# Graph network of four layers on one core: layer 0 with its sums two blocks ahead of its lists, and gathers that wait for the fourth gather ahead

## The chip, the cores and the metric

The kernel runs on one core of a Trainium2 chip. The metric is the device time of one launch in microseconds; lower is better. A core has five instruction streams that run beside each other and meet through semaphores: PE (matrix products), DVE (VectorE), ACT (ScalarE), POOL (GpSimd, which here issues the gathers) and SP (which issues plain loads). Each stream is in program order.

## What is computed

There are 3327 nodes with 256 features and an adjacency matrix of 3327 x 3327 integers, about 16 ones in a row. Layer 0 is an attention whose score depends on the row alone, so that its softmax has only two weights in a row, one for neighbours and one for the others:

```python
h = x @ Wt.T + bt
s = leaky_relu(h @ Wa.T + ba, 0.2)
w = softmax(where(adj > 0, s, NEG), axis=1)
y = x + (w @ h) @ Wp.T + bp
x = gamma * (y - mean(y)) * rsqrt(var(y) + EPS) + beta
```

Layers 1 to 3 are transformer layers over the neighbours of each node, with eight heads:

```python
q, k, v = layer_norm(x) @ w_qkv
x = x + softmax(where(adj != 0, q @ k.T * SCALE, -inf)) @ v @ w_proj + b_proj
x = x + gelu(layer_norm(x) @ w1 + b1) @ w2 + b2
```

## The kernel before

The nodes are 26 blocks of 128 rows (the last has 127). Four consecutive blocks are a group; the seventh group has two. All engines' orders are written out by hand: what the Python code calls first comes first in each engine's stream.

**Layer 0** reads the adjacency matrix once and does two things with it. The first is the *lists*: of each row the numbers of its neighbours, at most 40. VectorE multiplies a block's row of zeros and ones with column numbers (`candidates`, one product and 16 searches for the eight largest of a segment), and then takes the largest of these (`list`, five searches and four replacements). The second is the *sums*: the sum of h over a row's neighbours, and their number. For it PE turns the block (`turn`: 26 transposes, which ScalarE copies back from PSUM in four pieces to `s_aT`), and two turned blocks at a time are multiplied with h, split into three bf16 parts (`Group.sums`, L843 and L845).

When a group's sums are complete, twelve steps follow: `copy` and `back` bring the sums back to rows (`s_acc`), `soft` takes the number of neighbours (`deg`, L882) and each node's place in an ordering by this number (`places`, `rank`) and the two softmax weights, `mix` and `project` give the update, `add` and `norm` the normalized row, `norm1`, `turn1`, `qkv` the first transformer layer's queries, keys and values, and `store` writes them. Keys and values go to `kv1`, in the order of the nodes, everything else to `t1`.

The order: block 0 is loaded and turned, then `setup` computes h of all nodes (`x_turn`, `h_of`), with VectorE and ScalarE sharing the copies. Then block i+1 is loaded and block i turned; after two blocks their sums are made; and the steps of a finished group wait in a list `late`, from which `some` takes one before `candidates`, one before `list` and one after it. A load's tail columns are cleared on GpSimd (L702), which at the start has 26 gathers of x in its stream. After the last block, the permutation `perm` that sorts the nodes by their number of neighbours is worked out from the ranks, in between the last group's steps.

**Layers 1 to 3** go through the blocks in the sorted order, so that a block's rows have about equally many neighbours. `gather_rows` (L1186) fetches a block's row of `t1`; `issue` (L1226) fetches keys and values of one neighbour of each of the 128 rows: one gather on GpSimd, 270 KB in layer 1 and 262 KB after it, up to four for one buffer, of which there are ten. A gather waits for its buffer, and for the completion of the eighth indirect transfer ahead of it, whose semaphore it uses again. VectorE makes scores from the keys (L1248, L1249) and weighs the values (L1289), PE adds these up (L1294) and does the dense part.

Of the kernel before, what the change touches and what calls it, by code (L numbers as in the profile page):

```python
# [17 lines left out]
P = 128  # L18
N = 3327
# [43 lines left out]
FAR = 2.0 ** 100  # L63

# [459 lines left out]
def sparse_path(ctx, tc, ins, out, dram, flag):  # L524
# [98 lines left out]
    with tc.tile_pool(name="a", bufs=1) as a, tc.tile_pool(name="aw", bufs=2) as aw, \  # L623
# [42 lines left out]
        nrow = 3 * D + 2 * H0 + 1  # L666
        row = a.tile([1, nrow], FP, name="s_row")
        o = 0
        for name, n in (("gamma", D), ("beta", D), ("bp", D), ("bt", H0), ("Wa", H0), ("ba", 1)):
            src = ins[f"L0_gnn_{name}"]  # L670
            nc.sync.dma_start(row[:, o:o + n], src if len(src.shape) == 2 else src[None, :])
            o += n
# [15 lines left out]
        places = a_acc.tile([P, 512], FP, tag="places", name="places")  # L688

        class Block:  # L690
# [5 lines left out]
            def load(self):  # L696
                i, r = self.i, self.r
                a32 = aw.tile([P, N], I32, tag="a32", bufs=3, name=f"s_a32_{i}")
                for p0, p1 in (((0, P),) if r == P else ((0, r // 16 * 16), (r // 16 * 16, r))):
                    nc.sync.dma_start(a32[p0:p1], ins["adj"][i * P + p0:i * P + p1, :])  # L700
                self.abf = aw.tile([P, PADDED], BF, tag="abf", bufs=3, name=f"s_abf_{i}")
                nc.gpsimd.memset(self.abf[:, N:], 0.0)  # L702
                if r < P:
                    nc.gpsimd.memset(self.abf[96:P, :], 0.0)
                nc.scalar.sign(self.abf[:r, :N], a32[:r])
# [11 lines left out]
            def candidates(self):  # L717
                i = self.i
                v = aw.tile([P, NSEG, SEG], BF, tag="v", name=f"s_v_{i}")
                nc.vector.tensor_mul(v, self.abf.rearrange("p (s c) -> p s c", c=SEG),  # L720
                                     seg1[:, None, :].to_broadcast([P, NSEG, SEG]))
                self.cand = aw.tile([P, NSEG, 8], FP, tag="cand", name=f"cand_{i}")
                for s in range(NSEG):
                    nc.vector.max(out=self.cand[:, s, :], in_=v[:, s, :])  # L724
# [15 lines left out]
        def setup():  # L740

            wtT = a.tile([P, 2, H0], FP, name="s_wtT")
            S.wpT = a.tile([H0, D], FP, name="s_wpT")
# [5 lines left out]
            nc.vector.tensor_copy(wtT, pt[:, :2 * H0].rearrange("p (c h) -> p c h", c=2))  # L749
            nc.vector.tensor_copy(S.wpT, pt2[:H0, :D])  # L750
# [7 lines left out]
            S.gam_b, S.bet_b, S.bp_b = (brow[:, k * D:(k + 1) * D] for k in range(3))  # L758
            bt_b = brow[:, 3 * D:3 * D + H0]
            wa_b = brow[:, 3 * D + H0:3 * D + 2 * H0]  # L760
            ba_b = brow[:, nrow - 1:nrow]

            h_sb = aw.tile([P, NB, H0], FP, tag="abf", bufs=3, name="s_h")
            nc.vector.memset(h_sb[96:P, NB - 1, :], 0.0)
            turned = {}

            def x_turn(g):
                blocks = GROUPS[g]
                xT = aw.tile([P, 2, 512], FP, tag="hT", name=f"s_xT_{g}")
                for c in range(2):  # L770
                    pb = bank(f"s_px_{g}_{c}")
                    for j, i in enumerate(blocks):
                        nc.tensor.transpose(pb[:, j * P:(j + 1) * P],
                                            x_sb[:, i, c * P:(c + 1) * P], ident)
                    (nc.vector.tensor_copy if c else nc.scalar.copy)(
                        xT[:, c, :len(blocks) * P], pb[:, :len(blocks) * P])
                turned[g] = xT

            def h_of(g):
                blocks, xT = GROUPS[g], turned.pop(g)  # L780
                ph = bank(f"s_ph_{g}").rearrange("p (b h) -> p b h", h=H0)
                for j, i in enumerate(blocks):
                    for c in range(2):
                        nc.tensor.matmul(ph[:, j, :], xT[:, c, j * P:(j + 1) * P],
                                         wtT[:, c, :], start=(c == 0), stop=(c == 1))
                full = [j for j, i in enumerate(blocks) if ROWS[i] == P]
                for j0, j1, r in ((0, len(full), P), (len(full), len(blocks), ROWS[-1])):
                    if j1 > j0:
                        i0 = blocks[j0]
                        nc.vector.tensor_add(  # L790
                            h_sb[:r, i0:i0 + j1 - j0, :], ph[:r, j0:j1, :],
                            bt_b[:r, None, :].to_broadcast([r, j1 - j0, H0]))

            for g in range(len(GROUPS)):
                x_turn(g)
                if g:
                    h_of(g - 1)
            h_of(len(GROUPS) - 1)

# [3 lines left out]
            nc.vector.tensor_copy(hs[:, :, :H0], h_sb)  # L805
            nc.vector.tensor_sub(rest, h_sb, hs[:, :, :H0])
            nc.vector.tensor_copy(hs[:, :, H0:2 * H0], rest)
            nc.vector.tensor_sub(rest, rest, hs[:, :, H0:2 * H0])
            nc.vector.tensor_copy(hs[:, :, 2 * H0:3 * H0], rest)
            S.fold = a.tile([P, H0], FP, name="s_fold")  # L810
            nc.vector.tensor_copy(S.fold, ident[:, :H0])
            nc.vector.tensor_add(S.fold, S.fold, ident[:, H0:])

            ph = bank("s_phsum")
            for i in range(NB):
                r = ROWS[i]
                nc.tensor.matmul(ph[:, :H0], ones[:r, :], h_sb[:r, i, :],
# [4 lines left out]

            nc.vector.tensor_mul(rest, h_sb, wa_b[:, None, :].to_broadcast([P, NB, H0]))
            s = S.s = a.tile([P, NB], FP, name="s_s")
            nc.vector.tensor_reduce(s, rest, AX.X, ALU.add)
            nc.vector.tensor_scalar(s, s, ba_b, None, ALU.add)
            nc.vector.scalar_tensor_tensor(s, s, 0.2, s, ALU.mult, ALU.max)

        class Group:
# [17 lines left out]

            def steps(self):
                return [self.copy, self.back, self.soft, self.mix, self.project, self.add,
                        self.norm, self.norm1, self.turn1, lambda: self.qkv(0),  # L850
                        lambda: self.qkv(2), self.store]
# [19 lines left out]
            def soft(self):  # L871
# [4 lines left out]
                def sv(name):  # L876
# [10 lines left out]
                                        top[:, :, None].to_broadcast([P, n, nd]), ALU.is_equal)  # L887
                for j in range(n):
                    i = b0 + j
                    nc.tensor.matmul(places[:, :nd], tri, OH[:, i, :], start=(i == 0), stop=True,  # L890
                                     skip_group_check=True)
                    t = aw.tile([P, nd], FP, tag="place", name=f"place_{i}")
                    nc.vector.tensor_mul(t, places[:, :nd], OH[:, i, :])
                    nc.vector.tensor_reduce(rank[:, i:i + 1], t, AX.X, ALU.add)
                    nc.tensor.matmul(places[:, :nd], rest_tri, OH[:, i, :], start=False, stop=True,
                                     skip_group_check=True)
# [36 lines left out]
            def project(self):  # L933
# [4 lines left out]
                nT = aw.tile([H0, 512], FP, tag="nT", bufs=1, name=f"s_nT_{g}")  # L938
                nc.scalar.copy(nT[:, :n * P], pt[:H0, :n * P])
                self.ps = []  # L940
                for j0 in range(0, n, 2):
                    ps = bank(f"s_pp_{g}_{j0}").rearrange("p (b d) -> p b d", d=D)
                    for j in range(2):
                        nc.tensor.matmul(ps[:, j, :], ones[0:1, :], row[:, 2 * D:3 * D],
# [623 lines left out]
```

## Time and profile before

| | us |
|---|---|
| time, median of three runs | 2890.99 (2877.77 to 2891.98) |
| span of the profiled run | 2886.5 |
| first row gather of layer 1 (L1186) starts | 630.1 |
| last gather of layer 3 starts | 2789.1 |
| VectorE busy in the whole span | 1981.0 |
| PE busy in the whole span | 2003.6 |
| GpSimd: 1344 gathers of keys and values, one of them | 1273.2, 0.947 |
| VectorE: 416 searches of `candidates`, one of them (L724) | 117.5, 0.360 |
| ScalarE: 104 copies of turned pieces, one of them (L715) | 83.3, 0.853 |

How to read it: the page gives each engine's busy time and, in 40 slices of 72 us, its busy share in tenths. A busy share tells little alone: an engine with 70% can be the bound of a stage if its work is in a chain with that of others. So the idle time matters, and what ended it: a row such as "DVE deg L882 <- ACT s_acc L869: 92.8, 6, 19.1" says that VectorE's instruction of line 882 was waited for in all 92.8 us, six times, 19.1 at most, until ScalarE's instruction of line 869 was done. In a timeline each row has its start, its duration, engine, line, operation, output and inputs, and in brackets the idle time before it and what ended it.

### The profile page before, as it was taken

The page shows a single profiled execution, that of the slowest core. Times are in us where ns is not written, and L with a number is a line of the kernel's source. Part 1 is how long each engine was busy: PE and PEld are TensorE (multiplying, and loading weights), DVE is VectorE, ACT ScalarE, POOL GpSimd, SP SyncE. Part 2 cuts the span into 40 slices and gives each one's busy share as a digit, 9 for nine tenths or more (in the row PEclk, how much of TensorE's full clock was granted, in tenths as well). Part 3 has the DMA queues.
Part 4 walks back from the last instruction along what each step waited for, and adds up shares of the span by engine and source line. Part 5 has one row for each costly group of instructions (what it writes and reads, how often), then busy time and mean ns, then how long its engine had stood idle before and what let it go on. Part 6 is the DMA issues. An engine that isn't in the chain of part 4 may idle for free. (4 is left out here: it accounts for less than half of the span.)

```text
span 2886.5 us, 21905 instructions
## 1 busy us (share of the span) xinstructions
PE 2003.6 (69%) x6391; PEld 1062.0 (37%) x6391; DVE 1981.0 (69%) x4141; ACT 791.8 (27%) x1363; POOL 1359.1 (47%) x1461
## 2 busy tenths in 40 slices
PE   4566666623678887897347878878782678777866
PEld 4344444411334333344213434333350233333334
DVE  2977787447787777773378877777714886778852
ACT  2443443200233332332102323332230023222221
POOL 3000000017776766650377655665405777777740
PEclk9677666756889989898678989988995798888988
DMA  4323331137776766670477656665506776666650
GB/s 179 128 98 119 125 104 52 52 112 217 217 220 197 210 197 188 181 180 16 144 210 210 194 174 178 190 181 155 120 27 189 210 202 194 190 190 188 200 135 15
DMA packets 144480, 453.67 MB, mean 157 GB/s; under 512 B 29522, under 2 KB 40157, under 8 KB 141022
## 3 DMA queue, kind: packets, MB, share of 16 engines
q0 software_dynamic: 113056, 370.26, 45.7%
q1 hardware_dynamic: 9834, 53.90, 5.3%
q10 hardware_dynamic: 21458, 28.02, 2.7%
q8 instruction: 52, 0.85, 0.1%
q14 instruction: 80, 0.65, 0.1%
HBM read 420.64 MB, written 31.42 MB: 157 GB/s over the span
## 5 line engine op out<-in xcount | busy, mean ns | idle before, releaser
L1226 POOL DMA_INDIRECT kv<-kv,t x1344 | 1273.2, 947 | 806.0 <-issue 370.0
L1294 PE MATMUL po<-vw,s_ident 128*128 128x512 f32 (+1 forms) x1380 | 778.2, 700 | 493.5 <-DVE vw L1289 443.6
L1248 DVE TENSOR_TENSOR kv<-kv,q 128x1024 f32<-128x1024 f32 (+3 forms) x363 | 413.4, 1139 | 309.7 <-DMA kv<-kv,t 152.9
L1294 PEld LDWEIGHTS po<-vw,s_ident 128*128 128x128 f32 x1380 | 286.3, 221 | 845.3 <-issue 476.5
L1249 DVE TENSOR_REDUCE sc<-kv 128x32 f32<-128x1024 f32 (+3 forms) x363 | 414.1, 1141 | 12.4
L1289 DVE TENSOR_TENSOR vw<-kv,w 128x1024 f32<-128x1024 f32 x333 | 371.2, 1127 | 0.2
L1373 PE MATMUL pu<-fT,s_w 128*128 128x512 f32 (+3 forms) x768 | 302.4, 527 | 1.0 <-ACT fT L596 1.0
L1396 PE MATMUL py<-gT,s_w 128*128 128x512 f32 (+2 forms) x672 | 283.8, 549 | 0.0
L1379 ACT ACTIVATE gT<-pu,pvb 128x512 f32<-128x512 f32 (+3 forms) x192 | 116.6, 608 | 350.7 <-PE pu L1373 350.2
L702 POOL MEMSET s_abf<- 128x1 bf16 x26 | 2.6, 104 | 435.2 <-PE s_ptb L714 251.6
L1373 PEld LDWEIGHTS pu<-fT,s_w 128*128 128x128 f32 x768 | 147.4, 201 | 136.2 <-issue 111.6
L1396 PEld LDWEIGHTS py<-gT,s_w 128*128 128x128 f32 x672 | 127.8, 192 | 123.1 <-issue 105.4
L714 PE MATMUL s_ptb<-s_ident_bf,s_abf 128*128 128x128 bf16 x676 | 76.5, 291 | 115.7 <-ACT s_aT L715 84.4
L724 DVE MAX8 cand<-s_v 128x8 f32<-128x208 bf16 x416 | 117.5, 360 | 0.9
L714 PEld LDWEIGHTS <-s_abf 128*128 128x128 bf16 x676 | 65.4, 135 | 128.9 <-issue 94.7
L1426 PE MATMUL pk<-s_w_qkv,nT 128*128 128x512 f32 x208 | 106.4, 636 | 8.8 <-ACT nT L596 8.8
L588 ACT ACTIVATE xn_f<-t,nm_f,rqy_f 128x256 f32<-128x256 f32 x78 | 42.9, 593 | 247.6 <-DVE nm_f L582 238.3
L1263 ACT ACTIVATE sc<-sc,mx 128x120 f32<-128x120 f32 (+6 forms) x78 | 31.9, 410 | 260.9 <-DVE mx L1260 257.1
L1334 DVE TENSOR_TENSOR t<-t,po 128x256 f32<-128x256 f32 x78 | 32.5, 417 | 99.7 <-PE po L1330 95.2
L715 ACT COPY s_aT<-s_ptb 128x896 bf16<-128x896 bf16 x104 | 83.3, 853 | 64.6 <-PE s_ptb L714 64.6
L1186 POOL DMA_INDIRECT t<-t,perm x26 | 24.6, 946 | 158.6 <-DMA colsb<-in_L_gnn_be_dram 151.0
L1414 DVE TENSOR_TENSOR t<-t,pd 128x256 f32<-128x256 f32 x75 | 29.5, 408 | 93.3 <-PE pd L1410 93.3
(285 smaller groups left out, 2455.0 us busy)
## 6 DMA issues: line engine op xcount, KB each, us to landing
s_a<-in_adj_dram SPq DMA_DIRECT2D x25, 1663.5 KB
kv<-kv,t POOLq DMA_INDIRECT x1344, 3.8
kv<-kvr ACTq DMA_DIRECT2D x52, 256.0 KB
kv<-s_kvr ACTq DMA_DIRECT2D x26, 256.0 KB
s_w<-in_L_gnn_w_dram SPq DMA_DIRECT2D x6, 1024.0 KB
t<-ql ACTq DMA_DIRECT2D x6, 592.0 KB
t<-s_x ACTq DMA_DIRECT2D x6, 512.0 KB
s_w_qkv<-in_L_gnn_w_qkv_dram SPq DMA_DIRECT2D x3, 768.0 KB
```

The costliest lines, as they stand in the source:

```text
L714: nc.tensor.transpose(pt[:, m, :], self.abf[:, k * P:(k + 1) * P], ident_bf)
L715: nc.scalar.copy(aT[:, k0:k0 + len(ks), :], pt[:, :len(ks), :])
L724: nc.vector.max(out=self.cand[:, s, :], in_=v[:, s, :])
L1226: nc.gpsimd.indirect_dma_start(out=t[:, s, :], out_offset=None, in_=kv[L], in_offset=bass.IndirectOffsetOnAxis(ap=t2[:, b, k:k + 1].bitcas ...
L1248: nc.vector.tensor_mul(k, k, self.q[b][:, None, :].to_broadcast([P, n, D]))
L1249: nc.vector.tensor_reduce(self.sc[b][:, s0:s0 + n, :], k.rearrange("p s (h d) -> p s h d", d=HD), AX.X, ALU.add)
L1289: nc.vector.tensor_mul(vw[:, :n * D].rearrange("p (s h d) -> p s h d", h=HEADS, d=HD), v, self.wp[b][:, s0:s0 + n, :, None].to_broadcast([ ...
L1294: nc.tensor.matmul(self.po[b][:, :m], ident, vw[:, s * D:s * D + m], start=(s0 + s == 0), stop=(s0 + s + 2 >= S), skip_group_check=True)
L1373: nc.tensor.matmul(c["pu", f][:, :n], w["w1"][:, e, f * P:(f + 1) * P], c["hT"][:, e, :n], start=(e == 0), stop=(e == 1))
L1379: nc.scalar.activation(g[:, :n], c.pop(("pu", f))[:, :n], AF.Gelu_apprx_tanh, bias=w["b1"][:, f:f + 1])
L1396: nc.tensor.matmul(c["py"][e][:, :n], w["w2"][:, f, e * P:(e + 1) * P], g[:, :n], start=(f == 0), stop=last)
L1426: nc.tensor.matmul(ps[:, :c1 - c0], c["hT"][:, e, j * P:(j + 1) * P], nxt["w_qkv"][:, e, c0:c1], start=(e == 0), stop=(e == 1))
```

## The change

In layer 0 blocks are loaded, signed and turned two blocks ahead of `candidates` and `list`, and a group's sums are made two blocks ahead. `setup` is cut into pieces: blocks 0 and 1 have their lists made before x is turned, and the lists of blocks 2 and 3 lie between the parts of h. The steps of the groups stand in a plan of half blocks (one slot before `candidates`, one before `list`), with room between a step on one engine and the next on another. The last group's steps stand among those of the permutation. Some steps are cheaper: bp is a 65th row of the projection, a group's four ranks are taken together, `norm` is on ScalarE, gamma and beta are applied to a whole group. Each gather of keys and values waits for the fourth one ahead of it. That is meant to keep VectorE at its lists while PE and ScalarE work ahead, and to keep fewer gathers in flight.

```diff
+FLIGHT = 4
+WAIT = mybir.DependencyInfo(mybir.DependencyClass.Sync, mybir.DependencyReason.DATA)
...
-                nc.gpsimd.memset(self.abf[:, N:], 0.0)
+                (nc.vector if i < 3 else nc.gpsimd).memset(self.abf[:, N:], 0.0)
...
                 for j in range(n):
                     i = b0 + j
-                    nc.tensor.matmul(places[:, :nd], tri, OH[:, i, :], start=(i == 0), stop=True,
-                                     skip_group_check=True)
-                    t = aw.tile([P, nd], FP, tag="place", name=f"place_{i}")
-                    nc.vector.tensor_mul(t, places[:, :nd], OH[:, i, :])
-                    nc.vector.tensor_reduce(rank[:, i:i + 1], t, AX.X, ALU.add)
-                    nc.tensor.matmul(places[:, :nd], rest_tri, OH[:, i, :], start=False, stop=True,
-                                     skip_group_check=True)
+                    add = [(tri, i)] + [(ones_bf, k) for k in range(b0, i)]
+                    if g:
+                        add += [(rest_tri, i - 4)] + [(ones_bf, k) for k in range(i - 3, b0)]
+                    for lhsT, m in add:
+                        nc.tensor.matmul(at[:, j, :], lhsT, OH[:, m, :], start=False, stop=True,
+                                         skip_group_check=True)
+                t = aw.tile([P, 4, nd], FP, tag="place", bufs=1, name=f"place_{g}")[:, :n]
+                nc.vector.tensor_mul(t, at[:, :n, :], OH[:, b0:b0 + n, :])
+                nc.vector.tensor_reduce(rank[:, b0:b0 + n], t, AX.X, ALU.add)
...
-                        nc.tensor.matmul(ps[:, j, :], ones[0:1, :], row[:, 2 * D:3 * D],
-                                         start=True, stop=False)
-                        nc.tensor.matmul(ps[:, j, :], nT[:, (j0 + j) * P:(j0 + j + 1) * P], S.wpT,
-                                         start=False, stop=True)
+                        nc.tensor.matmul(ps[:, j, :], S.nT[:, (j0 + j) * P:(j0 + j + 1) * P], S.wpT,
+                                         start=True, stop=True)
...
-                    nc.vector.scalar_tensor_tensor(xi, xi, self.n0.mv[:, j, 0:1], S.gam_b,
-                                                   ALU.subtract, ALU.mult)
-                    nc.vector.scalar_tensor_tensor(xi, xi, self.n0.rs[:, j:j + 1], S.bet_b,
-                                                   ALU.mult, ALU.add)
+                    nc.scalar.activation(xi, xi, AF.Identity, bias=self.n0.nm[:, j:j + 1],
+                                         scale=self.n0.rs[:, j:j + 1])
...
-        blk[0].load()
-        for i in range(NB):
-            if i + 1 < NB:
-                blk[i + 1].load()
+        for i in range(3):
+            blk[i].load()
+        for i in range(3):
+            blk[i].sign()
             turn(i)
...
+        for i in range(2):
             blk[i].candidates()
             blk[i].list()
+        S.w1 = load_qkv(1, a, bank)
+        weights0()
+        blk[3].load()
+        blk[3].sign()
...
+        split_h()
+        sums(1)
+        of_h()
+        turn(4)
+        sums(3)
+        groups[0].copy()
+        blk[5].load()
+        blk[5].sign()
+        turn(5)
+        sums(5)
+        names = ("copy", "back", "soft", "mix", "project", "add", "norm", "norm1", "turn1",
+                 "qkv0", "qkv2", "store")
...
+            at = dict(zip(names, (0, 1, 3, 4, 5, 6, 7, 8, 9, 10, 11, 12)))
+            first = 8 * g + 4
...
+        for i in range(4, NB):
+            if i + 2 < NB:
+                blk[i + 2].load()
+                blk[i + 2].sign()
+            for s in plan[2 * i]:
+                step(*s)
+            blk[i].candidates()
+            if i + 2 < NB:
+                turn(i + 2)
+                if i % 2 or i + 2 == NB - 1:
+                    sums(i + 2)
+            for s in plan[2 * i + 1]:
+                step(*s)
+            blk[i].list()
...
-                nc.gpsimd.indirect_dma_start(
+                got = nc.gpsimd.indirect_dma_start(
...
+                if len(self.flight) >= FLIGHT:
+                    tc.add_manual_dep(got.ins, self.flight[-FLIGHT].ins.name, WAIT,
+                                      reason="gathers in flight")
+                self.flight.append(got)
```

## The prediction

> **What bounds the kernel now.** I read the slices first, then VectorE's waits up to 640 us, then the timelines of the engines around the end of layer 0, then the gathers. From the page:
>
> ```profile
> DVE  2977787447787777773378877777714886778852
> POOL 3000000017776766650377655665405777777740
> PEclk9677666756889989898678989988995798888988
> ```
>
> One digit is 72 us. GpSimd starts its gathers in the ninth slice, so layer 0 is everything before; the timeline puts the first row gather (L1186) at 630.1 us. The rest, 630 to 2886 us, is layers 1 to 3. Busy time by stage of layer 0 (columns: stage, its length, then PE, weight loads, DVE, ACT, POOL, granted clock, DMA share, GB/s):
>
> ```profile
> 0.00:75.00 75.00, 34.70 (x257) 30.85 (x258) 21.44 (x41) 17.37 (x19) 28.64 (x41) 0.98 0.45 172
> 75.00:499.00 424.00, 266.51 (x1550) 192.28 (x1550) 331.21 (x1200) 182.41 (x208) 5.20 (x24) 0.68 0.30 106
> 499.00:567.00 68.00, 43.07 (x198) 27.24 (x197) 39.20 (x152) 19.91 (x32) 0.00 (x0) 0.70 0.10 36
> 567.00:630.00 63.00, 28.40 (x139) 17.65 (x137) 29.87 (x121) 8.30 (x20) 0.00 (x0) 0.67 0.16 51
> ```
>
> VectorE has the most work, 421.7 of 630 us, and idles 208; DMA never limits. Who ends its idle time:
>
> ```profile
> DVE deg L882 <- ACT s_acc L869: 92.8, 6, 19.1
> DVE s_wtT L749 <- PE s_pt_w L746: 35.9, 1, 35.9
> DVE s_x L955 <- PE s_pp L946: 21.0, 8, 5.0
> ```
>
> These are chains through other engines that VectorE, in program order, can only sit out: the sums of a group on PE, their copy and turn, then soft (L882); the first weights (L749); the projection (L955). The first comes six times, the longest here:
>
> ```profile
> 524.72 0.17 DVE L882 COPY deg<-s_acc 128x4 f32<-128x4 f32 x1 [19.08 <-ACT s_acc L869]
> ```
>
> In layers 1 to 3 GpSimd sets the pace where VectorE does not:
>
> ```profile
> 800.62 0.95 POOL L1226 DMA_INDIRECT kv<-kv,t  x1 [0.30 <-issue]
> 801.87 0.95 POOL L1226 DMA_INDIRECT kv<-kv,t  x1 [0.30 <-issue]
> ...
> DMA to landing us min/median/max: 3.3/3.8/10.9
> ```
>
> A gather every 1.25 us, 0.95 busy and 0.30 fixed. Layer 3's 448 gathers run from 2181 to 2789 us without a pause for a buffer. A gather lands 3.8 us after its start, so only three or four overlap.
>
> **What the Trainium skill says.** "PSUM — Partial Sum Buffer", Engine vs sequencer instructions: the queues of ScalarE, VectorE and GpSimd are strictly first in, first out. The trace agrees: candidates and lists that need nothing of PE stand behind L882 for 19.08 us. "DMA: Bandwidth & Descriptors", Anatomy of one DMA: about 2.0 us fixed plus bytes over 436 GB/s. A gather of 128 x 528 x 4 bytes is 270 KB: an estimate of 2.0 + 0.62 = 2.6 us after issue; the trace has 3.8 - 0.95 = 2.85, near it, and I use the trace. "TensorE: Matmul & The Clock Gate", The HAM clock gate: the clock is half unless PE has just been busy. The trace agrees in kind: 0.68 granted in layer 0, 0.85 in layer 1, where PE is busy 569 of 770 us.
>
> **The change, part by part.**
>
> *Less work on VectorE.* Seven copies of xT go to ScalarE: -4.6 us (L775). Ranks of a group are taken together: 26 x (0.20 + 0.20) = 10.4 us become 14 instructions of 164 elements at 0.33 (L885's size): -5.8. norm: 26 x (0.48 + 0.49) = 25.0 us become 12 instructions of 1024 elements at 1.22 (L1248's size) and two of 512 at 0.69 (L955): 16.0, so -9.0. Weight copies: -0.7. Together -20. ScalarE takes 26 x 0.59 (L588's size) + 4 + 1 = +20 on 228 of 630 us: hidden.
>
> *PE.* The bias goes into a 65th row of the projection: -31.6 us (52 of L944) as recorded. Ranks need 124 products with the triangles and ones plus one at the end instead of 52: +73 x about 0.2 = +14. PE drops from 373 to about 355 us.
>
> *The floor.* VectorE's 421.7 us, plus 26.6 us of gaps under 0.15 us between its instructions (summed from the trace), less 20, is 428. 2.4 us of that are constants done before block 0 is there; its sign ends at 14.5 us. Without any wait VectorE would finish layer 0 at 14.5 + 426 = 440. In the new tail the last group's norm1, turn, qkv and store come ahead of the permutation, so the store (14.5 us from the end of norm1 to the first gather, 615.6 to 630.1 before) overlaps 8 us of permutation and 3 of checks: first gather at 440 + 4 = 444. That is 186 us below 630: the most that the order can give.
>
> *What waits remain.* Start: blocks 0 to 2 are loaded and signed at once and their tails cleared by VectorE; before, block 1's tail sat behind 26 x gathers on GpSimd (to 38.5 us) and PE behind it, the 35.9 us. VectorE now does blocks 0 and 1 by 35 us and blocks 2 and 3 between the h additions. But PE has a queue: three turns of about 5 us (paced by ScalarE's four copies), the weights, x and turn 3 to about 77 us; VectorE waits some 16. Then splitting h (VectorE, to 84), and on PE sums 1 (6.5), hsum (6), turn 4 (5), sums 3 (6.5). Block 5's sign stands behind the copy of these sums on ScalarE: about 111 us, and candidates(5), free from 99, waits 12. Then turn 5, sums 5, back, turns 6 and 7, sums 7: the ranks of soft(0) come after all these on PE, about 143 us, while VectorE stands there from 118: 25. Sum of the start: 53. At 143 us VectorE is hardly ahead of before, where soft(0) ended at 131 and candidates(5) at 140; what it has gained is that PE is two blocks ahead.
>
> From there a group of four blocks costs VectorE 4 x 10.2 + soft 3.6 + mix 2.9 + add 6.3 + norm1 7.2 + store 0.2 = 61 us, and PE about 50 to 58 (turns 20, sums 12 to 16, group steps about 20). PE keeps up, with little to spare. copy, back and soft now lie half a block or more apart, so the L882 wait goes; what comes in its place is the rank products behind a turn and a sum on PE: about 5 us a group, five groups, 25. Tail: the last group's sums are done two blocks before the end; project to add and the permutation's products: 10. Sum: 53 + 25 + 10 = 88. First gather at 444 + 88 = 532, **98 us earlier**. Layers 1 to 3 start from the same state and are shifted.
>
> *The fourth gather.* The wait is attached to the gather on GpSimd; behind it stand only later gathers, row gathers and stores; VectorE's scores wait for them. A gather's fourth predecessor started 5.0 us before and landed after 3.8: 1.2 us to spare. From starts and landings in the trace, 39 of the gathers begin before their fourth predecessor has landed, by 61.2 us in all; in a run of such gathers only the longest counts if the others shift with it: 17 us over all runs, 12 of these at the ends of the three layers, where eight gathers take up to 10.9 us and the data's arrival, not the issue, sets the end. So 0 to 17 us, at worst 61; I take 4. About 38 gathers also carry a second DMA wait: nothing beside 0.30 us of fixed gap.
>
> Time: 2891 - 98 + 4 = **2797 us**.
>
> **The rivals.**
> - *VectorE flows almost freely* (waits of 30, not 88): with denser work PE's clock rises from 0.68 towards 0.85, the sums shrink, the queue at the start dissolves. For: PE's sums run at 0.21 us a product at the start of a group of them and at 0.11 later (timeline at 515 to 521). Against: PE's order at the start. 2891 - 156 + 4 = 2739.
> - *PE becomes the bound*: the transposes wait 84.4 us for ScalarE's copies (L714), and these stay; 44 (start of x) + 343 of work + 84 + some 105 of waits in PE's own order for norm1, signs and the tail = 576, first gather 54 earlier: 2841.
> - *Slower*: the gather wait costs at every gather, because handing over the landing takes longer than the 1.2 us to spare. 0.1 us more a gather is 134 us: 2891 - 98 + 134 = 2927. Against: no more than three or four are ever in flight except at the layers' ends.
> - *Nothing left*: start at 53 us of waits grows by another 90 since soft(0) waits for everything: 2891 +- 10.
>
> **How the numbers follow.** Forecast (2765 to 2825) 58%; free flow (2720 to 2765) 21%; PE bound (2825 to 2870) 13%; nothing left 4%; slower 4%. Range 2732 to 2848. Faster 0.92, same 0.04, slower 0.04.
>
> **What would show it.** First row gather at about 532 us; VectorE's wait for s_acc gone from 92.8 to under 15 and a wait of its rank product (place) for PE in its place, the longest about 25 us early on; the wait for the weights gone; layers 1 to 3 together within 15 us of 2256; gathers still 1.25 us apart, landing at 3.8. It would be wrong if VectorE waited over 130 us in layer 0, or if gathers came further apart than 1.25 us in layer 3.

## The result, and the profile after

| | before | after |
|---|---|---|
| time, median of four runs, us | 2887.26 (2877.77 to 2891.98) | 2786.99 (2780.46 to 2791.46) |
| ratio, 95% interval | 1 | 0.9655 (0.9621 to 0.9689) |
| first row gather of layer 1 starts, us | 630.1 | 515.8 |
| from there to the end, us | 2256.4 | 2262.8 |
| VectorE in layer 0: busy, idle in gaps over 0.15 us | 421.8, 181.8 | 402.3, 89.7 |
| PE in layer 0: busy, us | 372.7 | 328.3 |
| ScalarE in layer 0: busy, us | 228.0 | 243.6 |

The change is 100 us faster. All of it comes from layer 0, which is 114 us shorter by the two profiles; the three other layers became some us longer. Of the 114 us, 92 are idle time of VectorE and 20 its work. (The profile of the changed kernel is of its fastest run, 2780.5 us, so that the profiles differ by 108 us. By the means of several profiles further down, layer 0 is 111 us shorter and the rest 12 us longer.) The page of the changed kernel, the same three rows of tenths in slices, now of 69.5 us:

```profile
DVE  6597988578877877733788777777427878777852
POOL 4000000377766656602776575565017777767741
PEclk9768776678899888996788998898976889988988
```

VectorE has no empty start any more (its first digit was 2), and GpSimd's gathers begin in the eighth slice instead of the ninth. Busy time by stage (length, then PE, weight loads, VectorE, ScalarE, GpSimd, granted clock, DMA share, GB/s):

```profile
0.00:75.00 75.00, 35.16 (x271) 29.98 (x271) 51.41 (x161) 36.76 (x41) 32.05 (x42) 0.90 0.58 217
75.00:515.84 440.84, 293.16 (x1888) 221.92 (x1888) 350.86 (x1272) 206.84 (x270) 4.79 (x20) 0.74 0.31 107
```

In the first 75 us VectorE does 51.4 us of work, where it did 21.4: 30 us of lists that lay behind h before. In the rest of layer 0 it is busy for 350.9 of 440.8 us (80%; before 400.3 of 555.1, 72%). What ended VectorE's waits up to 560 us (in all, how often, the longest):

```profile
DVE place L909 <- PE places L906: 39.1, 7, 15.3
DVE s_v L734 <- ACT s_abf L717: 21.9, 2, 11.6
...
DVE s_h L807 <- PE s_ph L801: 9.6, 4, 3.8
...
DVE deg L892 <- ACT s_acc L879: 6.2, 1, 6.2
DVE s_x L984 <- ACT s_x L978: 6.0, 2, 5.4
DVE pf L1180 <- PE pp_perm L1176: 5.0, 1, 5.0
```

The wait for `s_acc` fell from 92.8 us in six waits to 6.2 in one, the 35.9 us for the weights are gone, and the rank product's wait for PE came in. The largest single waits in VectorE's timeline (the first row is block 5's product, the second group 0's ranks, the third the end of the permutation):

```profile
101.89 1.89 DVE L734 TENSOR_TENSOR s_v<-s_abf,seg 128x3328 bf16<-128x3328 bf16 x1 [11.60 <-ACT s_abf L717]
...
130.60 0.33 DVE L909 TENSOR_TENSOR place<-places,OH 128x164 f32<-128x164 f32 x1 [15.30 <-PE places L906]
...
511.37 0.21 DVE L1180 COPY pf<-pp_perm 128x52 f32<-128x52 f32 x1 [5.04 <-PE pp_perm L1176]
```

The gathers keep their pace. From the group of all 1344 and from GpSimd's timeline and waits:

```profile
DMA to landing us min/median/max: 3.2/3.7/8.1
...
689.83 0.95 POOL L1302 DMA_INDIRECT kv<-kv,t  x1 [0.30 <-issue]
691.08 0.94 POOL L1302 DMA_INDIRECT kv<-kv,t  x1 [0.30 <-issue]
...
POOL kv L1302 <- DMA kv<-kv,t: 88.9, 237, 3.0
```

They still start 1.25 us apart and the slowest now lands after 8.1 us (10.9 before). The last line counts the fixed gap of 0.30 us in each of its 237 waits, 71 us; so 88.9 - 71.1 = 18 us is what this line has of real waiting for a gather to land. Before, the same line had 103 waits of 0.30 us at most, and nothing beyond the fixed gap.

### The profile page after: what moved, and what is told of

The parts are those of the page before. It is cut to its first block, busy times and chain, and to the rows that moved or that the text cites. A ratio compares the mean times of both kernels' runs of the same rounds, so it can differ in the third digit from the quotient of the medians.

```text
span 2778.7 us, 21914 instructions
## 1 busy us (share of the span) xinstructions
PE 1949.8 (70%) x6409; PEld 1042.0 (38%) x6409; DVE 1962.2 (71%) x4061; ACT 807.6 (29%) x1398; POOL 1362.1 (49%) x1458
## 4 chain that ended last, share of the span: by engine, by line
PE 36%; DVE 31%; DMA 15%; issue 7%; POOL 7%; ACT 4%; DVEq 0%; ACTq 0%; SPq 0%; POOLq 0%
DMA kv<-kv,t 13%; PE po L1375 11%; PE pu L1454 7%; PE py L1477 6%; POOL kv L1302 6%; DVE kv L1329 6%; DVE vw L1370 5%; DVE sc L1330 5%; DVE cand L738 2%; PE s_pk L1008 2%; PE pk L1507 2%; PE po L1411 1%; PE s_pc L860 1%; PE s_pa L858 1%; DVE ctmp L751 1%
## 5 line engine op out<-in xcount | busy, mean ns | idle before, releaser
L1375 PE MATMUL po<-vw,s_ident 128*128 128x512 f32 (+1 forms) x1380 | 764.7, 689 | 508.1 <-DVE vw L1370 456.6
L726 PE MATMUL s_ptb<-s_ident_bf,s_abf 128*128 128x128 bf16 x676 | 70.3, 274 | 76.7 <-ACT s_abf L717 63.8
L726 PEld LDWEIGHTS <-s_abf 128*128 128x128 bf16 x676 | 59.2, 126 | 91.1 <-ACT s_abf L717 70.3
L1495 DVE TENSOR_TENSOR t<-t,pd 128x256 f32<-128x256 f32 x75 | 29.5, 408 | 88.9 <-PE pd L1491 88.9
L858 PE MATMUL s_pa<-s_aT,s_hs 128*128 128x256 bf16 x338 | 80.9, 287 | 13.2 <-DVE s_hs L820 13.2
L727 ACT COPY s_aT<-s_ptb 128x896 bf16<-128x896 bf16 x104 | 82.7, 858 | 19.9 <-PE s_ptb L726 19.7
```

Source lines behind the costliest of these rows:

```text
L726: nc.tensor.transpose(pt[:, m, :], self.abf[:, k * P:(k + 1) * P], ident_bf)
L858: nc.tensor.matmul(self.pa[:, c0:c0 + 2 * P], S.hs[:r, k, :P], aT[:r, k, :], start=(k == 0), stop=(k == NB - 1))
L1375: nc.tensor.matmul(self.po[b][:, :m], ident, vw[:, s * D:s * D + m], start=(s0 + s == 0), stop=(s0 + s + 2 >= S), skip_group_check=True)
```

## The experiments

Each is compared with the kernel before, run on the same chip. e1 to e4, e5 to e8 and e9 to e12 ran on three different chips, so runs on different chips are best compared by their ratios.

| run | time, us | ratio (95% interval) | first row gather | from there to the end |
|---|---|---|---|---|
| the change | 2786.99 | 0.9655 (0.9621 to 0.9689) | 515.8 | 2262.8 |
| e1, no gather wait | 2780.79 | 0.9619 (0.9605 to 0.9632) | 521.2 | 2259.6 |
| e2, before with the gather wait | 2898.4 | 1.0035 (1.0025 to 1.0045) | 630.2 | 2271.1 |
| e3, third gather | 2897.35 | 1.0024 (1.0011 to 1.0037) | 519.6 | 2375.5 |
| e4, second gather | 3538.64 | 1.2244 (1.2222 to 1.2265) | 518.1 | 3021.1 |
| e5, VectorE +49 us | 2815.24 | 0.9756 (0.9724 to 0.9788) | 549.5 | 2263.8 |
| e6, PE +33 us | 2809.0 | 0.9726 (0.9696 to 0.9756) | 540.6 | 2266.2 |
| e7, ranks later | 2768.75 | 0.9588 (0.9564 to 0.9613) | 495.7 | 2270.9 |
| e8, one block ahead | 2772.05 | 0.9601 (0.9571 to 0.9630) | 499.7 | 2270.1 |
| e9, before with tails on VectorE | 2877.99 | 0.9963 (0.9950 to 0.9976) | 616.9 | 2246.6 |
| e10, no room in the plan | 2787.86 | 0.9652 (0.9637 to 0.9667) | 515.4 | 2268.7 |
| e11, ranks later, block 5 early | 2764.56 | 0.9566 (0.9551 to 0.9582) | 494.3 | 2270.3 |
| e12, one ahead, ranks later, no gather wait | 2749.74 | 0.9517 (0.9504 to 0.9530) | 488.7 | 2260.6 |

The last two columns are from one profile each. Four profiles have the same layer 0 (the change, e1, e3, e4), and their first row gathers lie between 515.8 and 521.2, mean 518.7; below about 5 us such a difference says nothing.

### The gather wait: e1, e2, e3, e4

```diff
-FLIGHT = 4
+FLIGHT = 1 << 30
```

> The changed kernel without the added wait: a gather waits again only for the eighth indirect transfer ahead. Theory 'free': the wait costs what the traces show, so layers 1 to 3 (2262.9 us from the first row gather to the end in the changed kernel, 2256.4 in the kernel before) go back by 0 to 7 us, the kernel is 0 to 7 us faster than the changed one (ratio to before 0.963 to 0.966), and the last gathers of a layer land after about 10 us again in place of 7. Theory 'fewer in flight pays': layers 1 to 3 become longer by over 10 us, ratio 0.969 or more. Theory 'the wait costs at each gather': layers 1 to 3 shorter by over 20 us, ratio below 0.959.

In e2 the same wait is put into the kernel before, and nothing else:

```diff
-                nc.gpsimd.indirect_dma_start(
+                got = nc.gpsimd.indirect_dma_start(
...
+                if len(self.flight) >= FLIGHT:
+                    tc.add_manual_dep(got.ins, self.flight[-FLIGHT].ins.name, WAIT,
+                                      reason="gathers in flight")
+                self.flight.append(got)
```

> The kernel before with the fourth-gather wait and nothing else. 'Free': within 7 us of before, ratio 0.999 to 1.003, layer 0 as before (first row gather at 630). 'Fewer in flight pays': ratio below 0.997. 'Costs at each gather': ratio over 1.007.

The wait has a cost and no gain. e2 is 0.35% above the kernel before, 7 to 13 us by its interval, between what was set down for "free" and for a cost at each gather; e1 is 6 us below the changed kernel by their medians, with overlapping intervals. The column "from there to the end" says the same: with the fourth gather's wait it is 2262.8 to 2270.9 us in seven profiles of this layer order (the change, e5 to e8, e10, e11; mean 2267.5), without it 2256.4, 2259.6, 2246.6 and 2260.6 (before, e1, e9, e12; mean 2255.8). The profile of e9 is of its fastest run, 13 us below its median; without it the second mean is 2258.9. So the wait costs some 6 to 12 us.

> The changed kernel with a wait for the third gather ahead: that one started 3.75 us before and lands after 3.7, and in the changed kernel no gather started less than 0.26 us after the landing it waited for. If latency against pace is the whole matter ('free'), a gather takes (3.7 + 0.26) / 3 = 1.32 us in place of 1.25 where GpSimd sets the pace: 448 x 0.07 = 31 us in layer 3, less in layers 1 and 2, together 40 to 90 us more than the changed kernel: 2825 to 2880. If the wait were of no account at this depth either: within 10 us of 2787.

> A wait for the second gather ahead. 'Free at four' as latency against pace: (3.7 + 0.26) / 2 = 1.98 us a gather, 1344 x 0.73 = 981 us more at most, less what layers 1 and 2 have in hand; layer 3, which GpSimd bounds, from 705 to about 1030 us; in all 3450 to 3750 us. If latency falls well below 3.7 with two in flight, less: at 3.3 (the least in the trace of before) 1.78 us a gather and 3250 to 3450.

With `FLIGHT = 3` and `FLIGHT = 2` GpSimd's waits for a landing, first e3 and then e4:

```profile
POOL kv L1302 <- DMA kv<-kv,t: 236.1, 376, 5.3
```

```profile
POOL kv L1302 <- DMA kv<-kv,t: 1126.1, 998, 6.3
```

Less the fixed 0.30 us of each wait that is 123 and 827 us of waiting, and layers 1 to 3 grew by 108 and 754 us over the mean with four. A simple sum of two numbers of the traces comes near these sizes. The median gather lands 3.7 us after its start (3.4 in e4), and no gather starts less than 0.26 us after the landing that it waits for, be that of the fourth one ahead (the change), the third (e3) or the second (e4). With at most F in flight, a gather can then start every (landing + 0.26) / F us: 3.96 / 4 = 0.99, under the 1.25 us of issue; 3.96 / 3 = 1.32, 0.07 over it, times 1344 is 94; 3.66 / 2 = 1.83, 0.58 over it, times 1344 is 780. With four, a gather of median landing never waits, and what costs are the gathers that land late.

That the sum comes near is in part luck. e3 was expected at 40 to 90 us and took 108; e4 fell into its range. In layer 3 alone the sum gives e3 448 x 0.07 = 31 us, but from the first to the last gather of the layer e3 takes 681 us where the change takes 614, 67 us more; layers 1 and 2 take 25 and 23 us more, less than the sum. And in e4 the median distance from start to start is 1.99 us, not 1.83. A median landing leaves out the late ones, and a wait in one place can hide behind another; how much each of these does was not measured.

### Which engine sets the pace of layer 0: e5, e6

e5 repeats VectorE's product in `candidates`; e6 adds 338 products with h whose results are overwritten:

```diff
-                    nc.vector.tensor_mul(v, self.abf.rearrange("p (s c) -> p s c", c=SEG),
-                                         seg1[:, None, :].to_broadcast([P, NSEG, SEG]))
+                    for _ in range(2):
+                        nc.vector.tensor_mul(v, self.abf.rearrange("p (s c) -> p s c", c=SEG),
+                                             seg1[:, None, :].to_broadcast([P, NSEG, SEG]))
```

> The changed kernel, with VectorE's product of abf and the column numbers (1.88 us, 26 times) made twice: 49 us more on VectorE in layer 0, nothing else changed. Theory 'VectorE sets layer 0': 35 to 49 us more, first row gather at 550 to 565 (515.8 in the changed kernel); the waits for rank products shrink by what is missing from 49. Theory 'PE and ScalarE set layer 0': under 20 us.

```diff
+                for k in range(NB):
+                    r = ROWS[k]
+                    nc.tensor.matmul(self.pa[:, c0:c0 + 2 * P], S.hs[:r, k, :P], aT[:r, k, :],
+                                     start=True, stop=True)
                 for k in range(NB):
```

> The changed kernel with 338 more products of 256 columns on PE in the sums (13 times 26, overwritten by the real ones after): 37 us at 0.11 us each, 71 at 0.21. 'VectorE sets layer 0': it shows only through the start and the rank products, 10 to 25 us more, and VectorE's wait for rank products (39.1 us) grows by about as much. 'PE sets layer 0': 37 us or more.

VectorE was busy 451.1 us in place of 402.3, and the first row gather came 31 us after the mean of the undosed ones (549.5 - 518.7): of 49 us 31 show, and the rest went into waits that shrank (VectorE's idle gaps fell from 89.7 to 73.6 us). That is a little under what was set down for "VectorE sets layer 0". PE was busy 361.1 us in place of 328.3, and 22 of these 33 us show (540.6 - 518.7), inside what the same theory gave for e6. 16 of them are a longer wait for the rank products, 55.5 us in place of 39.1:

```profile
DVE place L913 <- PE places L910: 55.5, 7, 19.5
```

Two thirds of a dose on either engine reach the end. So neither bounds layer 0 alone. What fits both is that they hold each other up in turns, so that a wait taken away is partly given back.

### The rank products: e7, e11

In e7 the reading of a group's ranks (`t`, `rank`, the last product) becomes a step of its own, three slots after `soft`, which alone made VectorE stand behind PE's queue:

```diff
-                t = aw.tile([P, 4, nd], FP, tag="place", bufs=1, name=f"place_{g}")[:, :n]
-                nc.vector.tensor_mul(t, at[:, :n, :], OH[:, b0:b0 + n, :])
-                nc.vector.tensor_reduce(rank[:, b0:b0 + n], t, AX.X, ALU.add)
...
+            def ranks(self):
+                g, n, b0 = self.g, self.n, self.blocks[0]
...
-            at = dict(zip(names, (0, 1, 3, 4, 5, 6, 7, 8, 9, 10, 11, 12)))
+            at = dict(zip(names, (0, 1, 3, 6, 4, 5, 6, 7, 8, 9, 10, 11, 12)))
```

> The changed kernel with VectorE's two rank instructions of a group three half-blocks after soft (the last two groups: one or two), so that VectorE no longer stands behind turn and sums on PE; the products stay where they are on PE. 'VectorE sets layer 0, and the rank wait is on its path': the 39.1 us of waits for rank products fall below 5 and first row gather comes 15 to 35 us earlier (what was waited at the start, 15.3 us, may come back as a wait for a sign or for s_acc): 2752 to 2772. 'The wait only moves': within 8 us of the changed kernel.

The place wait of 39.1 us is gone altogether, and the first row gather is 20 us earlier than in the change (23 earlier than the mean of the four). About half of the wait came back as gain; some of the rest turned into waits further down the group's chain. In e7:

```profile
DVE s_x L974 <- PE s_pp L965: 9.9, 4, 7.8
...
DVE s_z L941 <- ACT s_m L922: 6.4, 2, 4.4
```

e11 has e7's order and, besides, block 5 loaded and signed before h is split:

```diff
         blk[3].load()
         blk[3].sign()
+        blk[4].load()
+        blk[5].load()
...
+        blk[5].sign()
         split_h()
```

> The changed kernel with the ranks read three slots after soft (as in the run with the ranks later, 2769 us, first row gather at 495.7) and, besides, block 5 loaded and signed ahead of the splitting of h, so that its sign does not stand behind the copy of group 0's sums on ScalarE. In the changed kernel VectorE's product of block 5 waits 11.6 us for that sign. Theory: VectorE, free of both, moves up by 8 to 12 us: first row gather 486, time 2759 (0.956). Rival: PE is the later one by then, and VectorE waits the same 12 us for h or for block 6's sums further on: first row gather 496, 2769 (0.959).

Block 5's wait is gone, but the first row gather moves only from 495.7 to 494.3. VectorE takes the time up a block later, at group 0's sums:

```profile
DVE deg L890 <- ACT s_acc L877: 12.6, 1, 12.6
```

So the rival was right: at the start PE is the later one, and the 11.6 us on block 5's sign were VectorE's wait for PE under another name. The time differs from e7's by less than the intervals are wide.

### What the lead and the room are worth: e8, e10

e8 turns and sums one block ahead in place of two; the plan's steps move by two slots so that the distance from sums to soft stays. With this, block 5's sign, turn and sums leave the start, and what remains of the last two groups' steps comes behind the last list. The main lines of the edit:

```diff
-            if i + 2 < NB:
-                turn(i + 2)
-                if i % 2 or i + 2 == NB - 1:
-                    sums(i + 2)
+            if i + 1 < NB:
+                turn(i + 1)
+                if i % 2 == 0 or i + 1 == NB - 1:
+                    sums(i + 1)
...
-            first = 8 * g + 4
+            first = 8 * g + 6
```

> The changed kernel with turns and sums one block ahead of the lists in place of two, and the groups' steps one block later in the plan, so that the last group's soft, mix and project and the group before's add to turn1 come after the last list. 'Two blocks ahead is what takes the waits away': VectorE waits longer for signs, sums or ranks in each group and at the end; the first row gather comes 25 to 60 us later (540 to 575). 'Room in the plan and the start do it, the second block does not matter': only the tail, under 20 us later.

One block ahead is faster than two, 499.7 against 515.8, where both theories had it later. With less of turns and sums in PE's queue ahead of the rank products, the place waits shrink, group 0's from 15.3 to 5.5 us and group 2's from 12.6 to 3.9, and `s_acc` does not appear among the waits:

```profile
DVE place L909 <- PE places L906: 20.8, 7, 5.5
...
DVE s_x L984 <- ACT s_x L978: 12.0, 2, 8.7
```

e10 keeps the lead of two and takes the room out of the plan for groups 1 to 5: one block of VectorE's work from sums to soft, as before.

```diff
-            at = dict(zip(names, (0, 1, 3, 4, 5, 6, 7, 8, 9, 10, 11, 12)))
-            first = 8 * g + 4
+            at = dict(zip(names, range(12)))
+            first = 8 * g + 3
```

> The changed kernel, with the room in the plan taken out for groups 1 to 5: copy in the slot right after the sums, back, soft, mix and the rest each in the next slot, so that one block of VectorE work (10.2 us) lies between the issue of the sums and soft, as in the kernel before, in place of two blocks. The two blocks' lead of PE stays. Theory that the room takes away the wait for s_acc: turn 5, sums 6.5, copies and the turn back about 5, in all 16 us on PE and ScalarE against 10.2 us of work on VectorE: 6 us of waiting more for each of five groups, VectorE's wait for s_acc at 30 to 40 us in place of 6, first row gather 545, time 2817 (0.976). Rival, that the lead of two blocks does it: wait for s_acc under 10 us, first row gather 516 to 521, time 2787 (0.965).

```profile
DVE place L909 <- PE places L906: 25.0, 7, 15.0
...
DVE deg L892 <- ACT s_acc L879: 5.6, 1, 5.6
```

The first row gather stays at 515.4, and the wait for `s_acc` is 5.6 us, once. (The place waits fall by 14 us, and 13.9 us of waits for the projection come in their place.) So the room in the plan is not what takes the wait for `s_acc` away. What differs between the kernel before and all of these is shown by PE's order. Before, around the 19.08 us wait (VectorE's soft started at 524.72):

```profile
494.81 3.72 PE L991 MATMUL s_pk<-s_w_qkv,s_hT 128*128 128x512 f32 x4
...
506.58 1.03 PE L991 MATMUL s_pq<-s_w_qkv,s_hT 128*128 128x256 f32 x4
507.44 0.94 PE L714 MATMUL s_ptb<-s_ident_bf,s_abf 128*128 128x128 bf16 x14
...
514.39 0.42 PE L843 MATMUL s_pa<-s_aT,s_hs 128*128 128x256 bf16 x1
...
522.27 0.44 PE L864 MATMUL s_pback<-s_ident,s_sc 65*128 65x65 f32 x2 [1.05 <-ACT s_sc L858]
```

The queries, keys and values of the previous group (12.8 us), a turn (7.0) and the group's sums (6.8) stand in this order ahead of its turn back, and the first of these can start only when VectorE has done `norm1` of the previous group. After, the turn back of a group comes ahead of these:

```profile
340.83 0.63 PE L876 MATMUL s_pback<-s_fold,s_sa 128*128 128x64 f32 x2
347.97 1.18 PE L594 MATMUL s_pn<-s_ident,xn_q 128*128 128x128 f32 x4 [6.51 <-ACT xn_q L591]
...
351.25 3.78 PE L1008 MATMUL s_pk<-s_w_qkv,s_hT 128*128 128x512 f32 x4 [0.66 <-ACT s_hT L599]
```

This order does not come from the lead. It comes from the plan: twelve steps in half-block slots take six blocks, while a new group is complete every four, so `back` of a group stands ahead of `qkv` of the one before it. In the kernel before, `some` took three steps a block, and a group was through with all twelve before the next one's sums were complete. The change, e8 (a lead of one block) and e10 (no room) all have the plan, and in none of them is the wait for `s_acc` left over 7 us. That the order is the cause is a reading of the traces: neither the plan without a lead nor the kernel before with its sums moved ahead was run, so what the plan and the lead are each worth stays open.

### The start: e9

The kernel before with only the tails of blocks 0 to 2 cleared on VectorE:

```diff
-                nc.gpsimd.memset(self.abf[:, N:], 0.0)
+                (nc.vector if i < 3 else nc.gpsimd).memset(self.abf[:, N:], 0.0)
```

> The kernel before, with the tails of blocks 0 to 2 cleared on VectorE, as in the change; nothing else moves. In its profile the last piece of block 0's turn waited on PE for GpSimd's clearing until 38.5 us, the weights and all parts of x stood behind it, and VectorE idled 35.9 us. Theory: of these only some 17 us can be had back, since the last parts of h also need the last of the 26 gathers of x, which lands at about 41 us; h is done at about 45 instead of 62 us, the first row gather comes at about 613 instead of 630, time 2870 (0.994), and the 35.9 us wait splits into one of about 15 for the weights and several of a few us for x. Rival A: all of it comes back: first row gather 595, time 2852 (0.988). Rival B: nothing, since VectorE then waits longer for block 1 or for the first group's sums: 630, 2887.

```profile
DVE deg L882 <- ACT s_acc L869: 77.8, 5, 18.1
DVE s_wtT L749 <- PE s_pt_w L746: 19.0, 1, 19.0
```

Of the 35.9 us 16.9 come back at once, and 13 of them reach the first row gather, 11 the time (0.9963). In the kernel before, this one line is thus worth a tenth of the gain of the change. Here the theory of 17 us was right on the start and 4 us too high on the end. Its trace shows a loss of this size on the way: the 52 products of `hsum` (L817) take 11.3 us at a granted clock of 0.50, where before they took 6.0 at 1.00. That these are the missing 4 us is not shown.

### A version that beats both: e12

> The version that the runs point to: blocks turned and summed one block ahead (alone 2772 us, first row gather 499.7), ranks read three slots after soft (alone 2769, 495.7), and gathers that do not wait for the fourth one ahead (alone 6 us better at the time). If the gains add where they do not take away the same wait: the ranks' wait was 20.8 us of the idle time with one block ahead, of which the half comes back, 10 us: first row gather 489, and 7 us from the free gathers: time 2755 (0.954). Rival: one block ahead and the later ranks cured the same wait, and what is left is PE's own work: first row gather 497, time 2763 (0.957).

e8, e7 and e1 together: 2749.74 us, 37 below the changed kernel and 139 below the kernel before. The first row gather, 488.7, is where the sum of the gains put it, and from there to the end it takes 2260.6. VectorE's waits in layer 0, after which no single cause is left over 13 us (of the first line 10 us are block 0's load and sign at the very start):

```profile
DVE s_v L734 <- ACT s_abf L717: 22.3, 2, 11.9
...
DVE s_h L807 <- PE s_ph L801: 12.7, 4, 5.8
DVE s_x L988 <- ACT s_x L982: 12.7, 2, 9.5
```

## Why the prediction was right, step by step

It said 2797 us and the time is 2787; it put the first row gather at 532 and the gain there at 98 us, and it is 515.8 and 114 (111 by the mean of the four profiles). The mechanism held in outline: layer 0's order, and the removal of waits on VectorE. Its steps:

- **Less work on VectorE**, -20: measured 421.8 to 402.3, -19.5. Held. ScalarE's +20 was 15.6, and hidden.
- **PE**, 373 to 355: measured 328.3. This term was mis-sized by 27 us, most of all in the ranks, which were to add 14 us at about 0.2 us a product. There are 120 products and one at the end in place of 52 (the forecast counted 124 and one), and yet they keep PE busy for only 4.5 us in place of 6.9. One product takes 0.18 us from start to end in both kernels, but before, VectorE's reading stood between those of two blocks, and now the twenty of a group start some 0.025 us apart. The first two lines are of before; the last two, of after, are the first and the last line of a group's twenty:

```profile
525.51 0.18 PE L890 MATMUL places<-OH,tri 128*128 128x41 bf16 x1 [1.24 <-DVE OH L885]
525.98 0.18 PE L895 MATMUL places<-OH,rest_tri 128*128 128x41 bf16 x1 [0.29 <-DVE place L893]
...
367.79 0.18 PE L906 MATMUL places<-OH,tri 128*128 128x41 bf16 x1
...
368.28 0.18 PE L906 MATMUL places<-OH,rest_tri 128*128 128x41 bf16 x1
```

The bias products (31.6 us) went as said, and the projection's other products took 23.0 us in place of 31.7, for a reason that no run shows. Of the work that stayed the same, the sums took 82.7 us in place of 89.1 and the turns 70.3 in place of 76.5, but the queries, keys and values took 85.6 in place of 81.3 and the turn back 18.1 in place of 13.1. PE's granted clock after 75 us was 0.74 in place of 0.68, with PE busy 66.5% of that stretch in place of 60.9%. This is the effect the "free flow" rival had named; the Trainium skill, "TensorE: Matmul & The Clock Gate", The HAM clock gate, ties the clock to how busy PE has just been, and the traces agree in kind. The two doses do so too: 0.72 where VectorE had more to do and PE was busy 63.5% (e5), 0.77 where PE had more to do and was busy 69.4% (e6). But what stayed the same took only some 3 us less in all, so a higher clock on the average is not what made the 27 us.
- **The floor**: "first gather at 440 + 4". VectorE's last instruction in layer 0 starts at 515.67 and the gather at 515.84; the +4 was nearly 0, so that the store was wholly hidden; the gather waits for VectorE (L1232) and not for the store. Without its 78 us of waits after block 0's sign the gather would have come at 438 (444 predicted).
- **What waits remain**, 88: measured 78. The start was 53, with "x additions 16", "block 5's sign 12" and "soft(0)'s ranks 25"; measured 9.6 for the additions, 11.6 for the sign, 6.2 for `s_acc` and 15.3 for the ranks, 42.7 together. The rank products, 25 over the later groups: 39.1 - 15.3 = 23.8. The tail, 10: 5.0 for the permutation and 6.0 for the last norm, 11.0. The sum held, and the longest wait is where it was said to be. Its parts held less well: in the later groups it is not about 5 us each but 12.6 us in group 2 and 0.6 to 4.1 in the others, and e11 shows that the wait for block 5's sign comes back as another one.
- **"copy, back and soft now lie half a block or more apart, so the L882 wait goes"**: it went, but the reason fails. In the kernel before, these steps also lay half a block apart, and with the room taken out again (e10) the wait stays away. By the traces it goes because the plan puts sums and turn back ahead of the previous group's queries, keys and values in PE's order; no run tests this alone.
- **"what it has gained is that PE is two blocks ahead"**: fails. One block ahead (e8) gains 16 us more. The second block lengthens PE's queue ahead of the ranks of groups 0 and 2, the largest waits for PE left in the change.
- **"PE keeps up, with little to spare"**: held. 33 us more of PE's work cost 22 (e6).
- **The start**: the 35.9 us wait was put down to block 1's tail, cleared behind the gathers of x. The tail was block 0's own, whose last transpose waited for it until 38.51 us, and it makes up 16.9 of the 35.9 us (e9), of which 13 reach the end of layer 0 in the order before.
- **The fourth gather**, 0 to 17, taken 4: e1, e2 and the profiles put it at 6 to 12. The term was mis-sized, inside its bounds: GpSimd waits 18 us for landings, and about half of that reaches the end.

The 10 us between forecast and time are thus: layer 0 is 13 us shorter than said (by the mean of the four profiles), the gather wait costs some 6 more than the 4 taken, and the median of before is now 4 below the one the forecast started from: -13 + 6 - 4 = -11. That two of these go against each other, and that the group's waits of 12.6 us and of under 5 add up to the 25 forecast, is luck.

Of the rivals, "free flow" was half right: it had a rise of the clock, but put the waits at 30 where 78 remained. "PE becomes the bound" is refused by e5, in which VectorE's dose still cost 31 of 49 us. "Slower" asked for 0.1 us more at every gather; that is what waiting for the third gather costs (e3, 108 us over 1344 gathers is 0.08), and waiting for the fourth does not come near it. "Nothing left" had soft(0) wait for everything, 90 us more; it waited 15.3 + 6.2.

## What to carry to other kernels

When two in-order engines hand work to and fro, ask what stands ahead of the awaited instruction in the other engine's queue, not how far the two are apart on the waiting engine: here the room on the waiting engine was worth nothing (e10), and a second block of lead cost 16 us (e8). A result that comes out of a busy queue is best read some steps after it was asked for (e7: a product and a sum moved, 18 us). A limit on transfers in flight costs little only if (time to landing + hand-over) divided by their number lies well below the time of an issue; even then those that land late cost something (6 to 12 us here), and near the limit the medians tell too little (e3). And a small product in a row of its like is not to be priced by its time from start to end (0.18 us here) but by the distance between starts (0.025 us).

## What the runs showed of the hardware that had not been expected

- A wait on a landing is handed on in 0.26 us at the least: no gather began sooner after the landing that it waited for, with four, three or two in flight. With the median landing of 3.7 us that puts four in flight at 0.99 us a gather, below the 1.25 us of issue, and three at 1.32, above it.
- Fewer gathers in flight hardly made each of them faster: the median landing is 3.8 us before, 3.7 in e1, with four and with three, 3.4 with two. Only the slowest landed sooner, 8.1 us against 10.9 before and 11.4 in e1.
- In the denser order some PE instructions became shorter and others longer: 287 ns against 301 for a product of the sums and 274 against 291 for a transposition of a block, but 733 against 713 for a product of the keys and values and 349 against 282 for one of the turn back (L874, before L864).
- The same 52 products of `hsum` took 275 ns each at a granted clock of 1.00 (before) and 421 ns at 0.50 (e9).
- Rank products of 41 columns start 0.025 us apart when nothing stands between them, while each takes 0.18 us from start to end.
